# The last expert block of a mixture-of-experts layer: its rows by a product with a gate matrix, and one image's gathers beside that block

## The chip, the cores and the metric

One core of one Trainium2 chip. The time is device microseconds of one execution, and of several runs the median. A profile is one further execution, recorded by the hardware profiler; its times are microseconds from the start of its span.

## The reference

Four images of 384 channels and 32 x 32 pixels pass two layers: attention with tables of relative positions and a feed-forward net (layer 0), then convolutions channel by channel and a mixture of experts (layer 1). The change touches the mixture alone:

```python
scores = jnp.einsum('bsd,de->bse', x, gate_w) + gate_b
probs = jax.nn.softmax(scores, axis=-1)
topk_vals, topk_idx = jax.lax.top_k(probs, TOP_K)
mask = jnp.sum(jax.nn.one_hot(topk_idx, NUM_EXPERTS, dtype=probs.dtype), axis=-2)
masked = probs * mask
masked = masked / (jnp.sum(masked, axis=-1, keepdims=True) + 1e-09)
h = jax.nn.gelu(jnp.einsum('bsd,edh->ebsh', x, w1) + b1[:, None, None, :], approximate=False)
y = jnp.einsum('ebsh,ehd->ebsd', h, w2) + b2[:, None, None, :]
out = jnp.einsum('bse,ebsd->bsd', masked, y)
...
t = t + _L1_ffn_ref(_ln_t(t), ...)
```

A pixel is a token. Each of the 4096 tokens goes to two of four experts (384 to 1536 to 384), and the two results come back to it weighted by its two gates and are added to it.

## The kernel before, in words

Attention comes first (`qkv_phase`, `attention_phase`, to about 1490 us). Everything else is `rest_phase`: for each image the projection, the net of layer 0, the convolutions, the gates, and the experts.

*Dispatch.* When an image's gates are known, `scatter` writes each token's normalised row twice into the DRAM tensor `xs_d`, sorted by expert, with indirect DMAs on GpSimd. The index of a row is in `pos`; the two gates of a token are in `gate`. Both are tiles of 128 partitions with 8 x 2 values: partition p and column j stand for token 128 j + p, the last index for the first and the second expert.

*Blocks.* An expert works on blocks of 128 rows. There are 67 in all (`ALL`), since the blocks of each expert are rounded up; which expert a block has is data, and its weights are fetched by index. The 67 are in four groups, one after each image, of 13, 16, 16 and 22. `blocks` (L1252) runs through a group. For block k `fetch` gathers 128 rows into `xg` (L1258), `turn` transposes them on TensorE and copies them to `xT` (L1271, L1272), and twelve times three products give `e_ps` (L1309), ScalarE applies the Gelu (`eh`, L1312) and one product adds to `y_ps` (L1287). `y_ps` has two buffers. VectorE adds the bias, which stands at the end of the second half's weights, into `yo` (L1290, two buffers), and SyncE stores `yo` to 128 rows of the DRAM tensor `y_d` (L1292).

*Weights.* A block uses two halves of 128 x 4998 floats each, `wts[block % 2][half]`, fetched by an indirect DMA (`weights`, L1277) on GpSimd three halves ahead. A half whose buffer already holds the right expert is not moved. The second half's buffer is free only when `yo` of the block two before has been made.

*Combine.* `result_rows` (L803) turns an image's ranks into rows of `y_d` and puts them into `pos`. `combine` (L1324) then runs through quarters of 256 tokens: `results` gathers four tiles of 128 rows from `y_d` (L1348), `weigh` scales one by its gate on ScalarE (L1360) and adds the other, scaled, on VectorE (L1361), and `finish` transposes the sums on TensorE into `out_ps` (L1337), adds them to the residual on VectorE (L1338) and stores the result (L1339). For images 0 to 2 this starts at block 6 of the last group (`NOT_LAST`), by which all of their rows are in `y_d`, and is taken in steps beside the blocks. The fourth image may have rows in any block, the last one too; so `combine([B - 1])` stands behind the last block, with the whole of `y_d` as the source of its sixteen gathers. Its residual is still in SBUF (`xb`).

*Order.* GpSimd issues its DMAs in one queue, in the order of its instructions, and so does SyncE. The order on each engine is set when the program is built: a scheduler places instructions by its own estimate of when they are ready, except where `pin` (`keep_in_program_order`) holds them. `more` (L1483) is called after each twelfth of a block and hands out the other work in small steps, by a count of costs (`clock`). The tile `img` (128 x 3 x 38 x 38 floats) holds the padded image for the convolutions; the fourth image's convolution is its last reader.

Of the kernel before, what the change touches and what calls it, by code (L numbers as in the profile page):

```python
# [51 lines left out]

NOT_LAST = (2 * (B - 1) * N + NEXP * (BLK - 1)) // BLK - sum(COUNTS[:-1])
MAXB = B * N // BLK
OUTSIDE = 1e6


# [745 lines left out]
def result_rows(nc, small, image, pieces):  # L803


    shape = list(image["mask"].shape)

    def new(shape, name):
        return small.tile(shape, F32, tag=f"p_{name}", name=f"p_{name}", bufs=1)

    pos, part, step = new(shape, "pos"), new(shape, "prod"), new([P, 1, NEXP], "step")
    nc.vector.tensor_tensor(pos, image["rank"], bcast(pieces[0][1].unsqueeze(1), 1, shape[1]), ALU.add)
    for (_, off0), (lo, off) in zip(pieces, pieces[1:]):
        nc.vector.tensor_tensor(step[:, 0, :], off, off0, ALU.subtract)
        nc.vector.tensor_tensor(part, image["rank"], bcast(lo.unsqueeze(1), 1, shape[1]), ALU.is_ge)
        nc.vector.tensor_tensor(part, part, bcast(step, 1, shape[1]), ALU.mult)
        nc.vector.tensor_tensor(pos, pos, part, ALU.add)
    row = new([P, shape[1], 2], "fpos")
    for i, pick in enumerate(chosen(nc, new, image["mask"])):
        nc.vector.tensor_tensor(part, pick, pos, ALU.mult)  # L820
        nc.vector.tensor_reduce(row[:, :, i : i + 1], part, AX.X, ALU.add)
    nc.vector.tensor_copy(image["pos"], row)


def block_list(nc, small, cst, group, parts, done):
# [73 lines left out]
        nc.vector.tensor_tensor(done, done, took[:, turn], ALU.add)  # L899


def rest_phase(tc, cst, x, ao_d, ins, xs_d, y_d, x2_d, out):

# [6 lines left out]
    with ExitStack() as es:  # L912
# [339 lines left out]
        def blocks(g, more):  # L1252

            xT, xgs = {}, {}

            def fetch(k):
                xg = ld.tile([P, C], F32, tag="xg", name="xg")
                load = nc.gpsimd.indirect_dma_start(  # L1258
                    xg, None, from_xs, bass.IndirectOffsetOnAxis(ap=g["slot"][:, k, :], axis=0),
                    bounds_check=NEXP * CAP - 1, oob_is_err=False,  # L1260
                )
                for other in g["after"]:
                    after(load, other)
                xgs[k] = xg

            def turn(k):
                xg = xgs.pop(k)
                t = work.tile([P, KC, BLK], F32, tag="xT", name="xT")
                ps = ps_y.tile([P, KC, BLK], F32, tag="t", name="xT_ps")
                for c in range(KC):  # L1270
                    nc.tensor.transpose(ps[:, c, :], xg[:, c * P : (c + 1) * P], ident)  # L1271
                nc.scalar.copy(t, ps)  # L1272
                xT[k] = t

            def weights(k, fh):
                w = wts[(g["start"] + k) % 2][fh]
                nc.gpsimd.indirect_dma_start(  # L1277
                    w, None, ins["w12"], bass.IndirectOffsetOnAxis(ap=g["row"][:, k, fh : fh + 1], axis=0),
                    bounds_check=NEXP * 2 * P - 1, oob_is_err=False,
                )  # L1280
                return w

            pend = []

            def second(k, ff, hs, w, py):
                o = WB + ff % FH * C
                nc.tensor.matmul(py, hs, w[:, o : o + C], start=(ff == 0), stop=(ff == NF - 1))  # L1287
                if ff == NF - 1:
                    yo = hid.tile([P, C], F32, tag="yo", name="yo", bufs=2)
                    nc.vector.tensor_tensor(yo, py, w[:, WB + FH * C :], ALU.add)  # L1290
                    n = (g["start"] + k) * BLK
                    nc.sync.dma_start(y_d[n : n + BLK, :], yo)  # L1292


            fetch(0)
            ws = {h: weights(*divmod(h, 2)) for h in range(3)}
            turn(0)
            for k in range(g["nb"]):
                py = ps_y.tile([P, C], F32, tag="y", name="y_ps", bufs=2)
                for ff in range(NF):  # L1300
                    fh, f = divmod(ff, FH)
                    h = 2 * k + fh
                    w = ws[h]
                    if ff == 0 and k + 1 < g["nb"]:
                        fetch(k + 1)
                    ph = ps_h.tile([P, BLK], F32, tag="h", name="e_ps")
                    for c in range(KC):
                        o = c * FH * P + f * P
                        nc.tensor.matmul(ph, w[:, o : o + P], xT[k][:, c, :], start=(c == 0), stop=(c == KC - 1))  # L1309
                    hs = hid.tile([P, BLK], F32, tag="eh", name="eh")  # L1310
                    o = KC * FH * P + f
                    nc.scalar.activation(hs, ph, AF.Gelu, bias=w[:, o : o + 1])  # L1312
                    pend.append((k, ff, hs, w, py))
                    if len(pend) > 2:
                        second(*pend.pop(0))
                    if f == 2 and h + 3 < 2 * g["nb"]:
                        ws[h + 3] = weights(*divmod(h + 3, 2))
                    if ff == NF // 2 and k + 1 < g["nb"]:
                        turn(k + 1)
                    more(k)  # L1320
            for p in pend:
                second(*p)

        def combine(bs):  # L1324


            w = 2 * P
            end = bs[-1] == B - 1
            y_rows = y_d if end else y_d[: (groups[-1]["start"] + NOT_LAST) * BLK]
            pieces = [p for g in groups for p in g["pieces"]]  # L1330

            def finish(b, n0, xr, zs):
                for c0, c1 in ((0, 2), (2, 3)):
# [7 lines left out]
            def results(b, n0):  # L1341

                zs = []
                for j in range(2):
                    ys = [new_row() for _ in range(2)]
                    for i, y in enumerate(ys):
                        index = images[b]["pos"][:, n0 // P + j, i : i + 1]
                        nc.gpsimd.indirect_dma_start(y, None, y_rows, bass.IndirectOffsetOnAxis(ap=index, axis=0))  # L1348
                    zs.append(ys)
                if end:  # L1350
                    return zs, xbs[b][:, :, n0 : n0 + w]
                t0 = b * N + n0
                xr = ld.tile([P, KC, w], F32, tag="xr", name="xr")
                nc.sync.dma_start(xr, x2_d[:, t0 : t0 + w].rearrange("(k p) n -> p k n", p=P))
                return zs, xr

            def weigh(b, n0, zs):
                for j, (z, y) in enumerate(zs):
                    gate = images[b]["gate"][:, n0 // P + j, :]
                    nc.scalar.activation(z, z, AF.Copy, scale=gate[:, 0:1])  # L1360
                    nc.vector.scalar_tensor_tensor(z, y, gate[:, 1:2], z, ALU.mult, ALU.add)  # L1361
                return [z for z, _ in zs]

            if not end:
                for b in (*bs, B - 1):
                    result_rows(nc, small, images[b], pieces)
                    yield 3.0, 0.0
            todo = [(b, n0) for b in bs for n0 in range(0, N, w)]
            ahead = {}
            for i, (b, n0) in enumerate(todo):  # L1370
                for more in todo[i : i + (len(todo) if end else 2)]:
                    if more not in ahead:
                        ahead[more] = results(*more)
                zs, xr = ahead[b, n0]
                for _ in range(0 if end else 5):
                    yield 0.3, 0.0
                zs = weigh(b, n0, zs)
                for _ in range(0 if end else 5):
                    yield 0.3, 0.1
                finish(b, n0, xr, zs)  # L1380

        xbs, marks = {}, {}

# [99 lines left out]
        def more(g, k):  # L1483
            clock[0] += 0.05
            clock[1] += 1.36
            if g is groups[-1] and k == NOT_LAST and "combined" not in g:
                g["combined"] = combine(range(B - 1))
            spend(g.get("combined", iter(())))
            while clock[0] < clock[1] and spend(todo):
                pass  # L1490

        for i, g in enumerate(groups):
            blocks(g, lambda k: more(g, k))
            if i + 1 < len(groups):
                while "after" not in groups[i + 1]:
                    next(todo)
        for _ in groups[-1]["combined"]:
            pass
        for _ in combine([B - 1]):
            pass  # L1500


# [1 line left out]
def metaformer_kernel(ctx: ExitStack, tc: tile.TileContext, ins, out):  # L1504
# [14 lines left out]
    ao_d = [dram.tile([C, B, YT * IMG], F32, name=f"ao_d{i}") for i in range(2)]  # L1519
    x2_d = dram.tile([C, NT], F32, name="x2_d")  # L1520
    xs_d = dram.tile([NEXP * CAP, C], F32, name="xs_d")
    y_d = dram.tile([ALL * BLK, C], F32, name="y_d")

    with tc.tile_pool(name="held", bufs=1) as pool:
# [3 lines left out]
        ]  # L1528
        qkv_phase(tc, cst, ins["x"], ins["w_qkv"], qk_d, v_d)
        attention_phase(tc, cst, held, ins["tabs"], ins["tv"], qk_d, v_d, ao_d, xs_d, list(range(HEADS)))  # L1530
    rest_phase(tc, cst, ins["x"], ao_d, ins, xs_d, y_d, x2_d, out)


def attn_tables(table_q, table_k, table_v):
# [68 lines left out]
```

## Time and profile before

| | |
|---|---|
| median of 3 runs | 3050.28 us (3049.36 to 3055.75) |
| profiled execution, own time | 3065.37 us |
| its span | 3063.6 us |
| mean granted TensorE clock | 0.977 |
| TensorE busy | 2923.0 us, 95% of the span |
| VectorE busy | 1960.3 us, 64% |
| ScalarE busy | 1369.9 us, 45% |
| GpSimd busy | 1150.8 us, 38% |
| DMA | 500.56 MB, mean 163 GB/s |
| last `yo` starts | 3031.21 us |
| gathers of the combine step | 64, about 0.96 us each on GpSimd |

A line of a timeline has the start, the duration, the engine, the line of the kernel, the operation and its tiles (out<-in), and in brackets how long the engine had been idle before it and what ended that. PE is TensorE, DVE VectorE, ACT ScalarE, POOL GpSimd, SPq SyncE's queue. A duration on SPq or POOL of a DMA is that of its issue, not of the transfer. In a table of windows each row is one stretch of time: its length, the busy time of each engine with the number of instructions, the granted clock, the busy share of the 16 DMA engines, and GB/s.

### The profile page before, as it was taken

The page shows a single profiled execution, that of the slowest core. Times are in us where ns is not written, and L with a number is a line of the kernel's source. Part 1 is how long each engine was busy: PE and PEld are TensorE (multiplying, and loading weights), DVE is VectorE, ACT ScalarE, POOL GpSimd, SP SyncE. Part 2 cuts the span into 40 slices and gives each one's busy share as a digit, 9 for nine tenths or more (in the row PEclk, how much of TensorE's full clock was granted, in tenths as well). Part 3 has the DMA queues.
Part 4 walks back from the last instruction along what each step waited for, and adds up shares of the span by engine and source line. Part 5 has one row for each costly group of instructions (what it writes and reads, how often), then busy time and mean ns, then how long its engine had stood idle before and what let it go on. Part 6 is the DMA issues. An engine that isn't in the chain of part 4 may idle for free.

```text
span 3063.6 us, 63474 instructions
## 1 busy us (share of the span) xinstructions
PE 2923.0 (95%) x25391; PEld 2018.1 (66%) x25391; DVE 1960.3 (64%) x3577; ACT 1369.9 (45%) x2833; POOL 1150.8 (38%) x1123
## 2 busy tenths in 40 slices
PE   9988999999999999999899789999999999999996
PEld 4545777777777777777533347776577767777775
DVE  3227787878787878787478879999899540001101
ACT  1115767666766666666312232433342343233332
POOL 1114646464747473747300212251124231124412
PEclk9998999999999999999999889999999999999998
DMA  4446676767666676665400305724243165356742
GB/s 158 139 134 199 156 222 158 220 159 217 166 212 170 203 177 203 171 209 153 171 21 34 142 19 191 275 108 152 100 162 126 34 227 220 138 219 249 263 183 73
DMA packets 274568, 500.56 MB, mean 163 GB/s; under 512 B 135632, under 2 KB 204112, under 8 KB 266592
## 3 DMA queue, kind: packets, MB, share of 16 engines
q1 hardware_dynamic: 186576, 272.29, 29.0%
q0 software_dynamic: 37792, 202.68, 17.9%
q10 hardware_dynamic: 49904, 21.53, 3.6%
q8 instruction: 200, 3.28, 0.5%
q14 instruction: 96, 0.79, 0.1%
HBM read 543.58 MB, written 152.37 MB: 227 GB/s over the span
## 4 chain that ended last, share of the span: by engine, by line
PE 74%; DVE 13%; issue 6%; DMA 3%; ACT 2%; POOL 2%; SPq 0%; another core or an unknown queue 0%; DVEq 0%; POOLq 0%; ACTq 0%
PE e_ps L1309 12%; PE y_ps L1287 12%; DVE xb L1097 8%; PE t_ps L406 8%; PE sc_ps L221 7%; PE av_ps L221 7%; PE tabq_ps L221 6%; PE qk_ps L174 4%; PE a_ps L416 4%; PE tv_ps L221 2%; PE v_ps L185 2%; PE proj_ps L985 1%; PE tabk_ps L221 1%; PE tap_ps L1145 1%; PE f_ps L1020 1%
## 5 line engine op out<-in xcount | busy, mean ns | idle before, releaser
L1309 PEld LDWEIGHTS e_ps<-xT,w 128*128 128x128 f32 x4824 | 656.4, 193 | 215.1 <-issue 12.2
L349 POOL TENSOR_TENSOR bias<-b,s 128x416 f32<-128x416 f32 (+24 forms) x656 | 659.9, 1042 | 176.6 <-DMA s<-sd 160.5
L1309 PE MATMUL e_ps<-xT,w 128*128 128x128 f32 x4824 | 670.7, 277 | 11.7 <-DVE xb L1038 5.0
L1287 PE MATMUL y_ps<-w,eh 128*128 128x384 f32 x1608 | 652.4, 491 | 15.6 <-ACT eh L1312 12.8
L1097 DVE SCALAR_TENSOR_TENSOR xb<-img,pack,xb 128x1024 f32<-128x1024 f32 (+1 forms) x539 | 634.6, 1241 | 0.0
L1312 ACT ACTIVATE eh<-e_ps,w 128x128 f32<-128x128 f32 x804 | 292.8, 367 | 724.3 <-PE e_ps L1309 665.3
L1277 POOL DMA_INDIRECT w<-in_w,row x134 | 169.2, 1263 | 743.6 <-PE y_ps L1287 276.8
L398 DVE TENSOR_REDUCE extra<-arow 128x32 f32<-128x32 f32 (+24 forms) x768 | 381.7, 556 | 9.0 <-ACT arow L387 5.4
L377 DVE CUSTOM_DVE_ANT_0 arow<-sc_ps,bias 128x1024 f32<-128x1024 f32 x256 | 312.8, 1222 | 101.3 <-issue 52.5
L387 ACT ACTIVATE arow<-arow,nm 128x1024 f32<-128x1024 f32 x256 | 302.2, 1180 | 77.0 <-DVE nm L377 66.8
L406 PEld LDWEIGHTS t_ps<-ident,arow 128*128 128x128 f32 x2048 | 220.4, 142 | 173.6 <-ACT aT L407 100.6
L407 ACT COPY aT<-t_ps 128x512 f32<-128x512 f32 x512 | 278.5, 603 | 92.8 <-PE t_ps L406 91.3
L406 PE MATMUL t_ps<-ident,arow 128*128 128x128 f32 x2048 | 282.3, 281 | 15.6 <-ACT arow L387 15.6
L1290 DVE TENSOR_TENSOR yo<-y_ps,w 128x384 f32<-128x384 f32 x67 | 37.0, 553 | 394.8 <-PE y_ps L1287 389.9
L221 PE MATMUL sc_ps<-kk,qs 48*32 48x512 f32 x4096 | 277.6, 605 | 6.6 <-DVE nm L377 5.6
L1287 PEld LDWEIGHTS y_ps<-w,eh 128*128 128x128 f32 x1608 | 248.3, 193 | 30.6 <-ACT eh L1312 17.2
L221 PEld LDWEIGHTS av_ps<-aT,vb 128*64 128x64 f32 x4096 | 222.3, 137 | 51.3 <-ACT aT L407 41.2
L221 PE MATMUL av_ps<-aT,vb 128*64 128x128 f32 x4096 | 237.7, 274 | 0.0
L314 DVE STREAM_TRANSPOSE b<-tabk_ps 128x480 f32<-128x480 f32 x256 | 218.5, 982 | 23.7 <-PE tabk_ps L221 22.2
L221 PE MATMUL tabk_ps<-tab,kq 48*128 48x480 f32 x512 | 223.3, 583 | 8.2 <-DVE b L314 8.2
L221 PE MATMUL tabq_ps<-tab,kq 48*128 48x480 f32 x512 | 220.4, 579 | 2.1 <-ACT aT L407 1.5
L318 ACT COPY st<-tabq_ps 128x480 f32<-128x480 f32 x256 | 142.3, 560 | 74.8 <-PE tabk_ps L221 46.3
(210 smaller groups left out, 3140.3 us busy)
## 6 DMA issues: line engine op xcount, KB each, us to landing
sd<-st SPq DMA_DIRECT2D x128, 480.0 KB
s<-sd SPq DMA_DIRECT2D x256, 240.0 KB
xs_d<-zero SPq DMA_DIRECT2D x64, 384.0 KB
tvw<-in_tv SPq DMA_DIRECT2D x120, 192.0 KB
y_d<-yo SPq DMA_DIRECT2D x67, 192.0 KB
qk_d<-qk_sb POOLq DMA_DIRECT2D x48, 256.0 KB
qs<-qk_d SPq DMA_DIRECT2D x256, 48.0 KB
kq<-qk_d ACTq DMA_DIRECT2D x56, 192.0 KB
```

Of the source, the lines that this page charges most:

```text
L221: ins = nc.tensor.matmul(*args, **kw)
L314: turn = nc.vector.transpose(b2.rearrange("p e y x -> p x (e y)")[:, i + j], ps[:, j, : SPAN * IMG])
L349: nc.gpsimd.tensor_tensor(bias[:, y0:y1, :], bass.AP(b2.tensor, b2.offset + (e * IMG + y0) * IMG, [list(b2.ap[0]), [(step * IMG + 1) * IMG ...
L377: nc.vector.tensor_tensor_reduce(s["flat"], ps.rearrange("p h n -> p (h n)"), s["bias"].rearrange("p y x -> p (y x)"), -SCALE, BIG, ALU.ad ...
L387: nc.scalar.activation(s["flat"], s["flat"], AF.Exp, bias=s["nm"], scale=-1.0, accum_out=dn[:, y % YT : y % YT + 1])
L398: pin(nc.vector.tensor_reduce(ex[:, i, :], a[:, p0:p1, :].rearrange("p y x -> p x y"), AX.X, ALU.add))
L406: pin(nc.tensor.transpose(pt[:, j, :], s["flat"][:, k0 : k0 + P], ident))
L407: pin(nc.scalar.copy(aT[:, 4 * g : 4 * g + 4, s["y"] % YB, :], pt))
L1097: ins_ = nc.vector.scalar_tensor_tensor(acc[:, k, y0:y1], img[:, k, dy + y0 : dy + y1, dx : dx + IMG], w7[:, k, dy, dx : dx + 1], acc[:, k ...
L1287: nc.tensor.matmul(py, hs, w[:, o : o + C], start=(ff == 0), stop=(ff == NF - 1))
L1309: nc.tensor.matmul(ph, w[:, o : o + P], xT[k][:, c, :], start=(c == 0), stop=(c == KC - 1))
L1312: nc.scalar.activation(hs, ph, AF.Gelu, bias=w[:, o : o + 1])
```

## The change

The last block's `yo` is not stored. All other blocks' rows are still gathered from `y_d`; only rows below `LAST` (66 x 128) count. A gather of a row at or above it is left out by a bounds check on the index, and its gate is set to zero in a copy of the gates, `kept`. The contribution of the last block reaches its tokens in another way: `picked` is a matrix of 128 rows (of the block) by 1024 tokens with a token's gate where that token's result is this row, and zero elsewhere. For a quarter of the image and each 128 channels, the product of `yo` and `picked` starts a sum in PSUM, to which the transposed weighted rows are added by products with the identity. An addition then takes the sum to the residual.

`picked` is made by `choose`: the distance of each token's row from `LAST` (`rel`) and the gates go as single floats to a small DRAM tensor `pick_d` of 4 x 1024, and come back broadcast over all partitions (512 KB each). One VectorE step of 128 x 1024 for each of the two experts compares the distance with the partition's number and multiplies by the gate, and a third adds the two. The four tiles of 1024 floats lie in `img`. `choose` is taken in steps with the quarters of images 0 to 2; in the built order its first VectorE steps follow the fourth image's `result_rows`, ahead of block 36's `yo`.

The sixteen gathers of the fourth image are issued once the last block but one has made its `yo`, that is in the program beside the last block. Weighing and the sums come after the last block, as before; the two instructions of `weigh` are pinned.

```diff
+LAST = (ALL - 1) * BLK
...
                     n = (g["start"] + k) * BLK
-                    nc.sync.dma_start(y_d[n : n + BLK, :], yo)
+                    g["result"] = k, yo
+                    if n < LAST:
+                        nc.sync.dma_start(y_d[n : n + BLK, :], yo)
...
+        kept = small.tile([P, nj, 2], F32, tag="e_kept", name="e_kept", bufs=1)
+        room = img.rearrange("p k y x -> p (k y x)")
+        picked, other, where, weight = (room[:, i * N : (i + 1) * N] for i in range(4))
+
+        def choose(row):
+            gate = images[B - 1]["gate"]
+            rel = small.tile([P, nj, 2], F32, tag="e_rel", name="e_rel", bufs=1)
+            nc.vector.tensor_scalar_add(rel, row, -float(LAST))
+            nc.vector.tensor_scalar(kept, rel, 0.0, None, ALU.is_lt)
+            nc.vector.tensor_tensor(kept, kept, gate, ALU.mult)
+            yield 0.5, 0.0
+            for i in range(2):
+                for j, src in enumerate((rel, gate)):
+                    nc.sync.dma_start(pick_d[2 * i + j].rearrange("(j p) -> p j", p=P), src[:, :, i])
+                yield 0.0, 0.0
+            for i in range(2):
+                for dst, j in ((where, 0), (weight, 1)):
+                    nc.sync.dma_start(dst, bass.AP(pick_d.tensor, pick_d.offset + (2 * i + j) * N, [[0, P], [1, N]]))
+                yield 0.0, 0.0
+                nc.vector.scalar_tensor_tensor(
+                    other if i else picked, where, pc["wrow"][:, 0:1], weight, ALU.is_equal, ALU.mult
+                )
+            nc.vector.tensor_tensor(picked, picked, other, ALU.add)
...
-            y_rows = y_d if end else y_d[: (groups[-1]["start"] + NOT_LAST) * BLK]
+            y_rows = y_d[:LAST] if end else y_d[: (groups[-1]["start"] + NOT_LAST) * BLK]
...
+            def close(b, n0, xr, zs):
+                yo = groups[-1]["result"][1]
+                sums = []
+                for c, (pool, tag) in enumerate(((ps_m, "m"), (ps_h, "h"), (ps_y, "y"))):
+                    ps = pool.tile([P, TOK], F32, tag=tag, name="out_ps", **({"bufs": 2} if tag == "y" else {}))
+                    nc.tensor.matmul(
+                        ps[:, :w], yo[:, c * P : (c + 1) * P], picked[:, n0 : n0 + w], start=True, stop=False
+                    )
+                    sums.append(ps)
+                for j in range(2):
+                    for c, ps in enumerate(sums):
+                        nc.tensor.matmul(
+                            ps[:, j * P : (j + 1) * P], zs[j][:, c * P : (c + 1) * P], ident,
+                            start=False, stop=(j == 1),
+                        )
+                for c, ps in enumerate(sums):
+                    nc.vector.tensor_tensor(xr[:, c, :], xr[:, c, :], ps[:, :w], ALU.add)
+                nc.sync.dma_start(out[b, :, n0 : n0 + w].rearrange("(k p) n -> p k n", p=P), xr)
...
-                        nc.gpsimd.indirect_dma_start(y, None, y_rows, bass.IndirectOffsetOnAxis(ap=index, axis=0))
+                        bound = {"bounds_check": LAST - 1, "oob_is_err": False} if end else {}
+                        nc.gpsimd.indirect_dma_start(
+                            y, None, y_rows, bass.IndirectOffsetOnAxis(ap=index, axis=0), **bound
+                        )
...
-                    gate = images[b]["gate"][:, n0 // P + j, :]
-                    nc.scalar.activation(z, z, AF.Copy, scale=gate[:, 0:1])
-                    nc.vector.scalar_tensor_tensor(z, y, gate[:, 1:2], z, ALU.mult, ALU.add)
+                    gate = (kept if end else images[b]["gate"])[:, n0 // P + j, :]
+                    keep = pin if end else lambda ins_: ins_
+                    keep(nc.scalar.activation(z, z, AF.Copy, scale=gate[:, 0:1]))
+                    keep(nc.vector.scalar_tensor_tensor(z, y, gate[:, 1:2], z, ALU.mult, ALU.add))
...
             spend(g.get("combined", iter(())))
+            if g is groups[-1] and g.get("result", (0,))[0] == g["nb"] - 2 and "tail" not in g:
+                for _ in g["combined"]:
+                    pass
+                g["tail"] = combine([B - 1])
+                next(g["tail"])
...
-        for _ in groups[-1]["combined"]:
-            pass
-        for _ in combine([B - 1]):
+        for _ in groups[-1]["tail"]:
             pass
```

## What was predicted, before the changed kernel had been run

> **What bounds the kernel now.** I read the timeline of the last 64 us first, because the change ends there, then the chain of waits over the same stretch; then the timelines of VectorE, GpSimd and SyncE around 2515 us, because the order of instructions in the two built programs puts the new preparation there; last a table of windows and the waits of SyncE's queue. The tail, by instruction:
>
> ```profile
> 3016.77 0.56 DVE L1290 TENSOR_TENSOR yo<-y_ps,w 128x384 f32<-128x384 f32 x1 [15.74 <-PE y_ps L1287]
> ...
> 3031.21 0.56 DVE L1290 TENSOR_TENSOR yo<-y_ps,w 128x384 f32<-128x384 f32 x1 [13.89 <-PE y_ps L1287]
> 3034.43 0.97 POOL L1348 DMA_INDIRECT rows<-y_d,pos  x1 [31.64 <-DMA y_d<-yo]
> ...
> 3053.43 0.96 POOL L1348 DMA_INDIRECT rows<-y_d,pos  x1 [0.30 <-issue]
> ...
> 3056.04 0.61 ACT L1360 ACTIVATE rows<-rows,gate 128x384 f32<-128x384 f32 x1 [1.86 <-DMA rows<-y_d,pos]
> ...
> 3057.24 0.62 DVE L1361 SCALAR_TENSOR_TENSOR rows<-rows,gate 128x384 f32<-128x384 f32 x1
> ...
> 3058.85 1.02 DVE L1338 TENSOR_TENSOR xb<-xb,out_ps 128x512 f32<-128x512 f32 x2 [0.99 <-PE out_ps L1337]
> ```
>
> TensorE bounds all but the end. After the last block's `yo` at 3031.21 come 32.4 us in which it is nearly idle. In them the store of `yo` must land before GpSimd may issue the first of 16 gathers (3.22 us after `yo` starts); the sixteen take 19.00 us from first to last start, 1.27 us each; and from the last one's start to the end it is 10.17 us. Two `yo` lie 14.44 us apart here.
>
> The second place, where the kernel is not short of anything that costs time yet:
>
> ```profile
> 2511.98 1.04 POOL L1277 DMA_INDIRECT w<-in_w,row  x1 [1.59 <-remote]
> ...
> 2514.21 0.19 DVE L821 TENSOR_REDUCE p_fpos<-p_prod 128x8 f32<-128x32 f32 x1
> 2519.26 0.56 DVE L1290 TENSOR_TENSOR yo<-y_ps,w 128x384 f32<-128x384 f32 x1 [4.87 <-PE e_ps L1309]
> ...
> 2521.00 1.05 POOL L1277 DMA_INDIRECT w<-in_w,row  x1 [0.30 <-issue]
> ...
> 2530.46 1.02 POOL L1258 DMA_INDIRECT xg<-xs_d,slot  x1 [0.30 <-issue]
> ...
> 2546.21 0.49 PE L1271 MATMUL xT_ps<-ident,xg 128*128 128x128 f32 x3
> ```
>
> ```profile
> 2516.00:2520.00 4.00, 4.00 (x27) 3.20 (x26) 0.56 (x1) 0.76 (x3) 3.09 (x4) 1.00 1.05 375
> ...
> 2536.00:2540.00 4.00, 4.00 (x26) 3.20 (x25) 0.64 (x2) 1.10 (x3) 1.00 (x1) 1.00 0.97 343
> ...
> 2548.00:2552.00 4.00, 4.00 (x27) 3.20 (x26) 0.00 (x0) 1.10 (x3) 0.00 (x0) 1.00 0.14 42
> ```
>
> The last two columns are the DMA engines' busy share and GB/s. From 2516 to 2546 the 16 DMA engines are full: a new expert begins at block 38, and four halves of weights of 2.5 MB each (blocks 38 and 39) pass, with scatters of 192 KB between. TensorE is still busy throughout, but with little margin: the rows `xg` of block 39, issued at 2530.46 behind two of these halves, landed by the single packets' records at about 2540, and are transposed at 2546.21.
>
> ```profile
> 2814.91 0.38 SPq L1339 DMA_DIRECT2D out<-xr  x1
> 2834.04 0.36 SPq L1354 DMA_DIRECT2D xr<-x_d  x1
> ```
>
> This is what a SyncE transfer meets in such a stretch: the load waits for the store ahead of it to land, which took 19 us for 24 packets of 1 KB per engine; between 2773.09 and 2776.77 the same pair took 3.7 us.
>
> **What the Trainium skill says.** "DMA: Bandwidth & Descriptors", section "Queues, rings and completion order": every DMA engine takes its queue rows in turn, packet by packet. The trace agrees: at 2812 to 2814 the records hold 33 weight packets of 19,992 bytes (about 0.7 us each) and 40 of SyncE's queue, one for one. The same page, "Why a DMA increments its semaphore by 16 and not by 1": one descriptor moves one contiguous run, so a store of single floats has a descriptor per float; no run here shows 4-byte data, but the loads of 128-byte runs at 48.9 us show 1536 packets in 1.22 us, 13 ns each per engine. "TensorE: Matmul & The Clock Gate", Part 1: the clock halves after an idle window of about 3.4 us; the windows table agrees (clock 0.66 in 3032 to 3036, then 0.50).
>
> **The tail, removed and moved.** The gathers of the fourth image no longer need the last block's store. They wait for block 65's, whose `yo` starts at 3016.77; GpSimd is free from 3002.8. First gather 3016.77 + 3.22 = 3019.99, last start 3038.99. They lie beside the last block, in windows where the DMA engines are all but idle (share 0.00 to 0.14), so it pays nothing. The scaling stays behind the last `eh` on ScalarE and the last `yo` on VectorE by program order.
>
> New work after `yo` ends at 3031.77: per quarter of the image three products of 128x256, six of 128x128, two weighings and three additions of 128x256. The products need `yo` and a buffer alone and start at once, about 0.2 us each (128x384 starts every 0.33); they lie beside the weighings. A quarter costs VectorE: two weighings 1.15 (starts 0.53 apart, the last 0.62), about 0.5 from the last weighing to the first sum (0.99 before, for a bank of four products at half clock), three additions 1.07 (the short one is 0.41): 2.75. If VectorE alone set the end: 3031.77 + 4 x 2.75 + 3.73 (end of the last addition 3059.87 to 3063.6) = 3046.5. The gathers are later: the last lands 3.1 to 3.9 after its start (first gather to first scaling 3.16; fifteenth 3.87), so with 3.8 the last weighing starts at 3042.8, ends 3043.4, additions 3044.0 to 3045.1, end 3048.8. **Gain 14.8**; bounds 14.4 (a pure shift by one block) to 15.5. The store dropped is off the path; the check on the indices is at 1.01 us for `xg` against 0.96, which the 0.3 us gaps absorb or 16 x 0.05 = 0.8 cost.
>
> **The preparation, added.** In the built order the three small VectorE steps (0.16 us each) follow the last reduction at 2514.21, and the first 128x1024 step stands before block 36's `yo` (2519.26). It waits for: positions ready 2514.6, two stores of 1024 single floats on SyncE's queue (64 packets per engine each), then a broadcast load of 512 KB. Behind it in VectorE wait `yo` of block 36, and behind that on GpSimd the weights of block 38's second half (2521.00 waits for this `yo`, since `yo` reads the bias in that buffer), two scatters, the first half of 39 and `xg` of 39. The two gate stores and the first load stand earlier, at 2495 to 2502, where the DMA share is 0.2 to 0.3: nothing.
>
> When does that first step go? The store starts about 2515.6 (1 us, as `yo`'s store shows). Until about 2525 GpSimd's queue still holds half of block 38 and six scatters: about 6 weight packets and 18 scatter packets per engine, so one for one 24 of the 64 floats pass. The other 40 then need 0.5 to 1.4 us (13 to 36 ns each, the spread of 128-byte packets), 2526; landing and SyncE's issue 2 us, the second store's 64 packets in front; 8 x 4 KB per engine at 0.16 us is 1.3; landing about 1: 2530.3. The step takes 1.24 (L1097, same shape): `yo` at about 2531.5, twelve us late. Its own buffer allows that, since `y_ps` has two and block 38 reuses it at 2538.
>
> GpSimd then issues the weights at 2532.4 instead of 2521.0, into empty engines: first packets 1.4 later, half 38 in 6.4 (128 packets at about 40 per 2 us), two broadcasts and `yo` beside it 2.7, scatters 1, half 39 in 6.4, `xg` 0.5 and landing 0.8: 2551.6, against its use at 2546.2. **TensorE waits about 5 us**, and since it is 100% busy from 2548 on, the loss stays. As a rule: stall = `yo` of 36 minus 2526. Bounds: 0 if the floats slip through and `yo` is back before 2526; 14 if a float costs 0.1 us per engine instead of 0.02, which puts 104 of them 8 to 10 us later.
>
> The second step waits for the second index load, issued behind the stall's own weights: 8 packets at 0.75 is 6 us, so block 37's `yo` goes at about 2545 instead of 2536.8; its weights are needed after 2566. Nothing. Later products, orders of ScalarE, GpSimd and the gathers of images 0 to 2 are the same instruction for instruction.
>
> Sum: -14.8 + 5 = -9.8. On the profiled execution, 3065.37 (span 3063.6 and 1.8 around it): 3055.6. The shown runs' median is 15.1 below that execution for a reason the profile doesn't show; I take the same difference from it: 3050.28 - 9.8 = **3040.5**.
>
> **Rivals.** *No stall* (the floats are passed several per turn, or `xg` has more margin than I read): for it, TensorE shows no stall in that stretch today; against it, the 19 us store. 3050.28 - 14.8 = 3035.5. *A longer stall that eats most of the gain* (9 to 21 us: floats at 0.06 to 0.15 us, or the delayed weights of block 38 late as well): 3044.3 to 3056, middle 3050. *Slower*: single-float stores to HBM cost over 0.15 us per engine each. The place is the wait of VectorE's first 128x1024 step ahead of block 36's `yo`; it decides once that `yo` is later than about 2547 (2526 + 14.8 + 6.1). At 0.2 us the 104 floats left at 2525 take 21, then 5 for load and step, and landing: about 2553, stall 27, 3062. For it: the same skill page, "Specifications", says that below 512 bytes the engine reads, modifies and writes; against it, 128 packets of 128 bytes to HBM at 322.95 took 0.52 us. *The gathers don't move* (they still wait for a later transfer): tail gain about 1, stall 5, 3054; the built order has them behind the last weights with seven queue semaphores to wait for, all of stores up to block 65, so little speaks for it.
>
> **How the numbers follow.** Forecast with a stall of 2 to 8.7: 0.46, own range 3037.5 to 3044. No stall 0.19; longer stall 0.20; slower 0.11; gathers unmoved 0.04. What this kernel's measurement can tell from no change is about 0.2%, 6.1 us. Faster by more: 0.46 + 0.19 = 0.65. Within: the longer stall and the unmoved gathers, 0.24. Slower: 0.11. The range starts at 3033, below the no-stall case with its best tail (3050.28 - 15.5, less the runs' own spread of some us), and ends at 3055, which leaves out the slower case and the very end of the two before it.
>
> **What would show it.** Right: first gather of the tail about 3.2 us after block 65's `yo`; 17.6 us instead of 32.4 from the last `yo` to the end, set by the last gather; block 36's `yo` 10 to 14 us late with VectorE idle on the load of `img` before it; a gap of about 5 us in TensorE ahead of the `xT_ps` group that stood at 2546. Wrong: no such gap, or one that begins at `y_ps` of block 38 instead; a tail set by VectorE; a change of the block period between 2750 and 2935.

## The result and the profile after

The change made the kernel slower: 3065.85 us median of 6 runs (3063.98 to 3073.9) against 3050.21 us (6 runs, 3049.36 to 3055.75), a ratio of 1.0053 with a 95% interval of 1.0041 to 1.0065, or 13 to 20 us. The profiled execution has a span of 3070.4 us and an own time of 3072.18.

First the timeline of the changed kernel's tail:

```profile
3036.59 0.56 DVE L1292 TENSOR_TENSOR yo<-y_ps,w 128x384 f32<-128x384 f32 x1 [15.74 <-PE y_ps L1289]
...
3039.89 1.01 POOL L1399 DMA_INDIRECT rows<-y_d,pos  x1 [17.27 <-DMA y_d<-yo]
...
3051.04 0.56 DVE L1292 TENSOR_TENSOR yo<-y_ps,w 128x384 f32<-128x384 f32 x1 [13.89 <-PE y_ps L1289]
...
3060.09 1.01 POOL L1399 DMA_INDIRECT rows<-y_d,pos  x1 [0.30 <-issue]
...
3063.83 0.62 DVE L1415 SCALAR_TENSOR_TENSOR rows<-rows,e_kept 128x384 f32<-128x384 f32 x1 [1.78 <-ACT rows L1414]
...
3065.34 1.27 DVE L1379 TENSOR_TENSOR xb<-xb,out_ps 128x256 f32<-128x256 f32 x3 [0.89 <-PE out_ps L1374]
```

The tail does what it was meant to do. The first gather comes 3.30 us after the `yo` of the last block but one, nine of the sixteen start before the last block's `yo`, and from that `yo` to the end it is 3070.4 - 3051.04 = 19.4 us where it was 32.4. So 13.0 us are gained there, and 13 to 20 us more than that must be lost elsewhere.

They are lost around block 36. SyncE's queue and VectorE in the changed kernel's timeline:

```profile
2501.24 1.43 SPq L1343 DMA_DIRECT2D pick_d<-gate  x2
2517.49 0.33 SPq L1347 DMA_DIRECT2D img<-pick_d  x1
...
2527.36 1.71 SPq L1343 DMA_DIRECT2D pick_d<-e_rel  x2
2548.13 9.72 SPq L1347 DMA_DIRECT2D img<-pick_d  x2
```

```profile
2527.16 0.17 DVE L1337 TENSOR_SCALAR e_rel<-p_fpos 128x16 f32<-128x16 f32 x1
...
2556.21 1.28 DVE L1349 SCALAR_TENSOR_TENSOR img<-img,pack 128x1024 f32<-128x1024 f32 x1 [28.21 <-DMA img<-pick_d]
2557.41 0.55 DVE L1292 TENSOR_TENSOR yo<-y_ps,w 128x384 f32<-128x384 f32 x1
2567.59 1.28 DVE L1349 SCALAR_TENSOR_TENSOR img<-img,pack 128x1024 f32<-128x1024 f32 x1 [9.62 <-DMA img<-pick_d]
```

A load from `pick_d` is issued once the store that it reads has landed. The first gate store, 4 KB, takes from 2501.24 to 2517.49 for that, while little else gets through (2 to 39 GB/s in windows of 4 us from 2500 to 2520). The two stores of positions land 20.7 and 24.9 us after their issue, at 2548.07 and 2552.70. Weights pass beside them at first. But by the records of the single packets no packet of any queue begins from 2544 to 2550, and still the stores haven't landed. A row of a table of windows, with the engines in the order PE, PEld (TensorE's loading of weights), DVE, ACT, POOL:

```profile
2544.00:2548.00 4.00, 4.00 (x27) 3.20 (x26) 0.00 (x0) 1.10 (x3) 0.00 (x0) 1.00 0.00 0
```

The load behind them lands 3.5 us after the second. VectorE stands idle for 28.21 us ahead of its first step over 128x1024, and block 36's `yo` waits behind it. What this does to TensorE, again by the timeline:

```profile
2518.98 1.65 PE L1289 MATMUL y_ps<-w,eh 128*128 128x384 f32 x2 [6.11 <-ACT eh L1316]
...
2558.11 1.62 PE L1289 MATMUL y_ps<-w,eh 128*128 128x384 f32 x2 [8.26 <-DVE yo L1292]
...
2571.42 1.65 PE L1313 MATMUL e_ps<-xT,w 128*128 128x128 f32 x6 [6.55 <-DMA w<-in_w,row]
...
2579.41 0.52 PE L1273 MATMUL xT_ps<-ident,xg 128*128 128x128 f32 x3 [1.28 <-DMA xg<-xs_d,slot]
```

Four gaps, 22.2 us. The last three belong to the late `yo`: a buffer of `y_ps` that it holds, weights that GpSimd may issue only after it, and the rows behind these. The first has nothing to do with `yo`. It comes right after the gate stores, and on ScalarE it begins with this:

```profile
2518.56 0.37 ACT L1316 ACTIVATE eh<-e_ps,w 128x128 f32<-128x128 f32 x1 [9.17 <-remote]
```

"remote" is a release that the profile finds in no instruction of this program. The three longer gaps also leave TensorE at half clock for a while (granted clock 0.50 from 2520 to 2524 and from 2556 to 2560, 0.54 from 2572 to 2576).

To compare kernels I use the starts of `yo` on VectorE: between two of them the same work lies in each kernel, whatever an execution lost before. The stretch from the `yo` of block 34 (counted from 0, as in the prediction) to the last one holds all of the change but the tail. Each figure of this kind is from one profiled execution.

### The profile page after: what moved, and what is told of

Its sections match the earlier page's. It is cut to its first block, busy times and chain, and to the rows that moved or that the text cites. A ratio compares the mean times of both kernels' runs of the same rounds, so it can differ in the third digit from the quotient of the medians.

```text
span 3070.4 us, 63606 instructions
## 1 busy us (share of the span) xinstructions
PE 2933.3 (96%) x25439; PEld 2027.1 (66%) x25439; DVE 1964.7 (64%) x3587; ACT 1372.5 (45%) x2833; POOL 1158.1 (38%) x1123
## 4 chain that ended last, share of the span: by engine, by line
PE 74%; DVE 13%; issue 5%; DMA 4%; POOL 2%; ACT 2%; SPq 1%; POOLq 0%; DVEq 0%; ACTq 0%
PE e_ps L1313 12%; PE y_ps L1289 12%; DVE xb L1099 8%; PE t_ps L407 7%; PE sc_ps L222 7%; PE av_ps L222 7%; PE tabq_ps L222 5%; PE qk_ps L175 4%; PE a_ps L417 3%; PE tv_ps L222 2%; PE v_ps L186 2%; PE tabk_ps L222 2%; DMA s<-sd 1%; PE proj_ps L987 1%; PE tap_ps L1147 1%
## 5 line engine op out<-in xcount | busy, mean ns | idle before, releaser
L1289 PEld LDWEIGHTS y_ps<-w,eh 128*128 128x128 f32 x1608 | 249.3, 193 | 33.9 <-ACT eh L1316 14.7
L1215 POOL DMA_INDIRECT xs_d<-rows,pos x64 | 78.6, 1229 | 259.9 <-DVE b_first L851 228.1
```

## The experiments

Ratios are against runs of the kernel before on the same chip in the same comparison. There its medians were 3051 to 3053 us with single runs from 3041 to 3061, so the ratio is the figure to read; 0.001 is 3.05 us.

| kernel | ratio, 95% interval | us from `yo` 34 to the last `yo` | against 543.77 |
|---|---|---|---|
| before, first profile | 1 | 560.77 | +17.0 |
| before, second profile | 1 | 543.77 | 0 |
| changed kernel | 1.0053 (1.0041 to 1.0065) | 573.57 | +29.8 |
| tail_only | 0.9945 (0.9926 to 0.9963) | 543.59 | -0.2 |
| prepare_only | 1.0085 (1.0064 to 1.0106) | 571.74 | +28.0 |
| late_steps | 0.9998 (0.9986 to 1.0010) | 553.42 | +9.7 |
| runs_64b | 0.9976 (0.9966 to 0.9986) | 551.96 | +8.2 |
| runs_late | 0.9975 (0.9961 to 0.9988) | 545.38 | +1.6 |
| rows_late | 0.9958 (0.9944 to 0.9972) | 543.98 | +0.2 |
| gate_floats | 1.0036 (1.0021 to 1.0051) | 553.93 | +10.2 |
| gate_spread | 0.9994 (0.9984 to 1.0003) | 543.76 | 0.0 |
| gate_pitch64 | 0.9999 (0.9988 to 1.0010) | 543.96 | +0.2 |

**The kernel before, once more.**

> The kernel before, for a second profile. All profiles since have the blocks 50 to 60 quicker by 13.4 us than the first profile of the kernel before, with the old tail and with the new one, and blocks 35 to 37 quicker by 4 where nothing is added. If that belongs to the one execution first profiled, this profile shows the quick blocks: from yo of block 50 to that of block 60 171.7 us instead of 185.1, from 34 to 38 78.7 instead of 82.4. If the kernel before is always so, it shows the same as the first.

The second profile shows the quick blocks (span 3043.1, own time 3044.89). The first had lost 17.0 us in this stretch that no later profile of any kernel loses. So the changed kernel's loss is measured against the second: 29.8 us. With the tail's 13.0 that makes +16.8, inside the 13 to 20 of the timed runs.

**Which half of the change costs?** tail_only:

```diff
-            for i in range(2):
-                for j, src in enumerate((rel, gate)):
...
-            nc.vector.tensor_tensor(picked, picked, other, ALU.add)
+            nc.vector.memset(picked, 0.0)
```

> The changed kernel without its preparation: the stores, loads and steps that build the matrix of gates are left out, and the matrix is set to zero, so the last block adds nothing to the fourth image; the moved gathers and the new products stay. Theory F (the loss lies in the preparation, in the stores of single floats): the tail keeps what its trace shows, 32.4 - 19.4 = 13.0 us, and nothing is lost at block 36: 3050.2 - 13.0 = 3037, between 3035 and 3039. Rival R (part of the loss lies in the moved gathers or in the new tail, not in the preparation): 3042 or more.

prepare_only: the kernel before with `pick_d`, `kept`, `choose` and this call of it, and nothing else of the change:

```diff
+                if not end:
+                    next(chooser, None)
                 zs, xr = ahead[b, n0]
```

> The kernel before with the preparation added and its result not used: the last block's rows are stored and gathered as before. Theory F: 26 us lost about block 36 and nothing won: 3076, between 3073 and 3080; the gate stores again take about 15 us until the load behind them is issued. Theory C (my prediction's: floats pass one for one with weight packets): a loss of 5 us, 3055, at most 3064. Rival R (part of the loss belongs to the moved gathers): between 3060 and 3072.

Both came out as theory F has it: 0.55% faster (17 us, interval 11 to 23), a little below the stated 3035 in its median of 3034.48, and 0.85% slower (26 us, 20 to 32; median 3076.89). The preparation carries the whole loss, and the moved gathers and the new products carry none.

**Late data, or blocked engines?** late_steps lets the same floats go out at the same places, but nothing on VectorE waits for them until block 55:

```diff
+            got = [room[:, i * N : (i + 1) * N] for i in range(4)]
...
+            key = small.tile([P, 1], F32, tag="e_key", name="e_key", bufs=1)
...
+            nc.vector.scalar_tensor_tensor(
+                key, groups[-1]["result"][1][:, 0:1], 0.0, pc["wrow"][:, 0:1], ALU.mult, ALU.add
+            )
...
-                    other if i else picked, where, pc["wrow"][:, 0:1], weight, ALU.is_equal, ALU.mult
+                    got[2 * i], got[2 * i], key, got[2 * i + 1], ALU.is_equal, ALU.mult
```

> The changed kernel with the same four stores of single floats, but the two steps over 128x1024 on VectorE stand some twenty blocks later, behind a later block's yo, and both pairs of rows have a place of their own. Theory H (the stores only make data late; the loss is VectorE waiting ahead of block 36's yo): that wait goes and all of the 26 us with it: 3037, at most 3040. Theory B (the stores also hold up everything else that the DMA engines write, and with it the other engines): the loss at the gate stores stays, 6 us of TensorE's stall and some at half clock, and the second pair of stores still holds up weights: 3043 to 3056.

Neither theory alone. The wait ahead of `yo` is worth 29.8 - 9.7 = 20 us, and 9.7 us stay without it, as theory B said. Its timeline shows where:

```profile
2490.73 1.43 SPq L1343 DMA_DIRECT2D pick_d<-gate  x2
...
2504.52 0.37 ACT L1316 ACTIVATE eh<-e_ps,w 128x128 f32<-128x128 f32 x1 [5.50 <-remote]
2506.98 4.64 SPq L1349 DMA_DIRECT2D img<-pick_d  x2
...
2515.27 1.22 SPq L1343 DMA_DIRECT2D pick_d<-e_rel  x2
2549.11 8.36 SPq L1349 DMA_DIRECT2D img<-pick_d  x2
...
2562.17 0.56 DVE L1292 TENSOR_TENSOR yo<-y_ps,w 128x384 f32<-128x384 f32 x1 [20.55 <-DMA y_d<-yo]
```

The second of the two loads at 2506.98 waits for the second gate store and is issued at 2511.29: that store took 19.5 us. About half of the 9.7 comes before block 36 (its `yo` is 5.4 us further from block 34's than in the second profile of before), behind the "remote" wait. The other half comes at block 38: its `yo` waits for the store of an earlier `yo`, which stands on SyncE's queue behind the loads that wait for the floats. The first of the two stores of positions took 33.8 us among the weights, the second 41.4; by the records of the packets, weights and floats pass about one for one there (40 of each from 2532 to 2534). Out of VectorE's way, the wait had gone into the next queue.

**The number of floats?** runs_64b writes 128 runs of 64 bytes twice, instead of 1024 single floats four times. The steps still stand ahead of a `yo`, but in the built order the first has moved by one block, from ahead of block 36's to ahead of block 37's:

```diff
+            for j, src in enumerate((rel, gate)):
+                nc.vector.tensor_copy(line[:, :, j, :], src.rearrange("p j i -> p i j"))
...
-                    nc.sync.dma_start(pick_d[2 * i + j].rearrange("(j p) -> p j", p=P), src[:, :, i])
+                nc.sync.dma_start(flat[i].rearrange("(p c) -> p c", p=P), line[:, i].rearrange("p s j -> p (s j)"))
```

> The changed kernel with the four stores of 1024 single floats made into two stores of 128 runs of 64 bytes (VectorE first puts a partition's positions and gates side by side), one load of 8 KB per partition for each of the two steps, and the steps ahead of block 36's yo as in the changed kernel. Theory F (the number of floats costs): the stores take below 2 us, the first step waits only for a load that passes weight packets, the stall is 0 to 6 us: 3037 to 3043. Theory Q (what makes the data late is SyncE's queue and the full DMA engines, not the floats): the stall stays at 15 us or more: 3052 or more.

```profile
2518.06 0.81 SPq L1346 DMA_DIRECT2D pick_d<-e_line  x2
2521.27 0.56 DVE L1292 TENSOR_TENSOR yo<-y_ps,w 128x384 f32<-128x384 f32 x1 [3.10 <-PE y_ps L1289]
2526.31 0.32 SPq L1351 DMA_DIRECT2D img<-pick_d  x1
...
2539.60 2.02 DVE L1354 SCALAR_TENSOR_TENSOR img<-img,pack 128x1024 f32<-128x1024 f32 x1 [17.77 <-DMA img<-pick_d]
2549.54 2.00 DVE L1354 SCALAR_TENSOR_TENSOR img<-img,pack 128x1024 f32<-128x1024 f32 x1 [7.92 <-DMA img<-pick_d]
...
2552.72 0.55 DVE L1292 TENSOR_TENSOR yo<-y_ps,w 128x384 f32<-128x384 f32 x1
```

Runs in place of floats take away 29.8 - 8.2 = 21.6 us of the loss, and the changed kernel turns into one faster than before (0.9976). A part of the 21.6 belongs to the shift, since block 36's `yo` at 2521.27 no longer waits. Ahead of it, the step would have held it until 2541.6, which is 2537.5 on the clock of the prediction; by the prediction's rule that is an estimate of 11.5 us lost instead of 8.2. Theory F's time is too low all the same: the first store took 8 us among the weights, not 2, and the first load (8 KB for each of 128 partitions) another 13 us from its issue to the step. This is the kind of wait that my prediction had described, and it costs 8.2 us here.

**The fourth corner.** runs_late has the runs of runs_64b and the late steps of late_steps. Both loads keep a place of their own, the steps work in place, and one copy on VectorE more puts the sum into the order of the tokens.

> runs_64b with its stores and loads at the same place and the steps over 128x1024 behind a later block's yo, as in late_steps. With the changed kernel, late_steps and runs_64b it fills the square of two causes: stores of floats or of runs, steps ahead of yo or behind. Theory H (what runs_64b still loses, some 8 us about blocks 36 to 39, is VectorE waiting ahead of yo): the loss goes, ratio 0.9957 as in rows_late, yo of 34 to 39 within 1 us of the kernel before. Rival Q (the broadcast loads among the weights delay weights and rows by themselves): 5 us or more stay, ratio 0.9972 or more.

By the trace 1.6 us stay, which is theory H: all but 1.6 of the 8.2 was VectorE waiting ahead of `yo`. What stays is for the most part one wait of TensorE for rows `xg` (1.34 us), issued among the loads. The timed ratio of 0.9975 lies on rival Q's side of the line that I had drawn. It stands for 7.6 us gained where the trace leads one to expect 13.0 - 1.6 = 11.4, and the interval (4 to 12) just reaches that. Whether runs_late loses something more that its one profile doesn't show stays open.

So the square is, in us lost: floats and early steps 29.8, floats and late steps 9.7, runs and early steps 8.2 (early by a block less), runs and late steps 1.6. The two causes are more than a sum, since the slower stores are, the longer the wait ahead of `yo`.

**What is it about the floats?** gate_floats is the kernel before with the two gate stores alone. gate_spread and gate_pitch64 send the same 2048 floats from the same places, 512 and 64 bytes apart instead of 4 (shown for 64, against gate_floats; 512 has 128 in place of the 16):

```diff
-                nc.sync.dma_start(pick_d[2 * i + 1].rearrange("(j p) -> p j", p=P), gate[:, :, i])
+                nc.sync.dma_start(
+                    pick_d[2 * i + 1].rearrange("(j p) c -> p j c", p=P)[:, :, 0:1], gate[:, :, i : i + 1]
+                )
...
-    pick_d = dram.tile([4, N], F32, name="pick_d")
+    pick_d = dram.tile([4, N, 16], F32, name="pick_d")
```

> The kernel before with nothing added but the two stores of the gates, 1024 single floats each, at the place where the changed kernel has them; nothing reads them. Theory F: the 2048 floats take about 14 us from their issue to the landing of the second, scatters' packets meanwhile take microseconds each, ScalarE waits 3 us or more on a release that is not from this core's program, and the kernel loses 5 to 9 us: ratio 1.0015 to 1.003. Theory C (13 to 36 ns per float): landed in 3 to 5 us, nothing lost, ratio within 0.001 of 1.

> As gate_floats, but the floats go to addresses 512 bytes apart instead of side by side. Theory F1 (a single float costs by itself): as slow as gate_floats, 14 us or more. Theory F2 (the cost comes from several DMA engines writing into the same short stretch of memory at once): landed in 5 us or less and nothing lost.

> As gate_spread with the floats 64 bytes apart instead of 512. Floats 512 bytes apart cost nothing and floats side by side cost about 11 us. If a stretch of 64 bytes is what engines must not share, this is as quick as gate_spread: landed in about 3 us, ratio within 0.001 of 1. If the stretch is longer (512 bytes, as the place where the Trainium skill's DMA page sets a limit for small descriptors), the loss stays in whole or in part: ratio 1.0015 or more.

DMA issues in 28 us from shortly before the stores (out<-in, queue, operation, count, KB each, median us from issue to landing), gate_floats first and then gate_pitch64:

```profile
y_d<-yo SPq DMA_DIRECT2D x1, 192.0 KB, 13.5
xs_d<-rows,pos POOLq DMA_INDIRECT x8, 11.2
```

```profile
xs_d<-rows,pos POOLq DMA_INDIRECT x13, 5.0
y_d<-yo SPq DMA_DIRECT2D x1, 192.0 KB, 2.1
...
pick_d<-gate SPq DMA_DIRECT2D x2, 4.0 KB, 2.9
```

And tables of windows, 4 us each, of gate_floats and of gate_pitch64:

```profile
2508.00:2512.00 4.00, 3.67 (x24) 2.81 (x22) 1.89 (x12) 0.20 (x1) 2.62 (x3) 1.00 0.55 17
2512.00:2516.00 4.00, 0.00 (x0) 0.00 (x0) 0.00 (x0) 0.00 (x0) 2.32 (x3) 1.00 0.63 22
2516.00:2520.00 4.00, 0.67 (x1) 0.50 (x2) 1.72 (x13) 1.00 (x3) 0.00 (x0) 0.59 0.81 71
```

```profile
2508.00:2512.00 4.00, 4.00 (x26) 3.20 (x25) 3.72 (x28) 1.15 (x4) 0.82 (x1) 1.00 0.19 71
2512.00:2516.00 4.00, 4.00 (x25) 3.17 (x25) 3.71 (x30) 1.17 (x4) 3.08 (x4) 1.00 0.37 128
2516.00:2520.00 4.00, 4.00 (x25) 3.15 (x24) 3.62 (x26) 1.15 (x4) 3.08 (x4) 1.00 0.41 150
```

The same floats, the same queue, the same moment. Side by side they cost 11 us (ratio 1.0036; 10.2 in the trace), more than the 5 to 9 expected; 64 or 512 bytes apart they land in 2.9 us and cost nothing. For the gate stores it is thus neither the number of floats nor their size, but their addresses. For the stores of positions this was not run by itself: runs_64b took away their number and their nearness together. In gate_floats a store of `yo` of 192 KB takes 13.5 us instead of 2.1, the DMA engines are 0.55 to 0.81 busy and move 17 to 71 GB/s, and for 4 us TensorE, VectorE and ScalarE all stand still, though SyncE alone has to do with these stores.

**A version that is faster than both.** rows_late takes floats and waits away:

```diff
+            nc.tensor.transpose(turned[: 4 * nj, :P], line.rearrange("p i s j -> p (i s j)"), ident)
+            rows = small.tile([4 * nj, P], F32, tag="e_rows", name="e_rows", bufs=1)
+            nc.vector.tensor_copy(rows, turned[: 4 * nj, :P])
+            nc.sync.dma_start(pick_d.rearrange("a (j p) -> (a j) p", p=P), rows)
```

> The changed kernel with another way to the same matrix of gates: VectorE puts positions and gates side by side, TensorE transposes the 32 columns, one store writes 32 runs of 512 bytes, two loads bring 8 KB per partition, and the three steps over 128x1024 stand behind a later block's yo, as in late_steps. Theory F+H (the loss is the stores of single floats and the wait that stands ahead of yo; both are gone here): only the tail's gain is left, about 13 us below the kernel before (ratio 0.9957; 0.994 to 0.997), and no gap over 1 us in TensorE in the stretch of blocks 35 to 39. Rival Q (any load of 512 KB broadcast over all partitions holds up weights): 5 us or more lost wherever the loads fall, ratio 0.998 or more.

```profile
2771.76 0.42 SPq L1348 DMA_DIRECT2D pick_d<-e_rows  x1
2775.72 0.81 SPq L1353 DMA_DIRECT2D img<-pick_d  x2
...
2853.19 2.48 DVE L1363 SCALAR_TENSOR_TENSOR img<-img,e_key 128x1024 f32<-128x1024 f32 x2
```

The ratio is 0.9958 (median 3038.73), 8.5 to 17 us faster than before, as expected; 0.2 us are lost on the way to the last `yo`. The loads are issued 4 us after the store, and the matrix is ready at 2857, 166 us before the first product with it. Store and loads stand some 250 us later than in the other kernels, but among other transfers too (DMA share 0.87 to 1.02 from 2772 to 2788). The loads of 1 MB each cost nothing here; rival Q, which had them cost 5 us wherever they fall, falls. What the transposition, the runs of 512 bytes and the later place are each worth, this kernel doesn't separate.

## Why the prediction was wrong

3040.5 us were predicted (range 3033 to 3055), and 3065.85 came. The rival called slower stood at 3062 with a chance of 0.11, and it came nearest: it had block 36's `yo` at about 2553. It put that down to the price of a single float, though, and floats 64 bytes apart cost nothing.

- *The tail: right, 1.8 us too good.* Predicted were 17.6 us from the last `yo` to the end, and it took 19.4. The gathers follow each other mostly at 1.31 us instead of 1.27 (some take 1.23 to 1.28 instead of 1.01), so the last starts 23.50 us after block 65's `yo` instead of 22.2; and the last sums begin 0.9 us after the weighing instead of 0.5 and take 1.27 instead of 1.07. The last gather sets the end, as predicted.
- *"The two gate stores and the first load stand earlier, at 2495 to 2502, where the DMA share is 0.2 to 0.3: nothing."* **This step failed.** Alone they cost 11 us (gate_floats). I had looked for other traffic that could hold them up, and never asked what they would hold up themselves.
- *"40 then need 0.5 to 1.4 us (13 to 36 ns each, the spread of 128-byte packets)".* **The same error in the other pair.** In the records the floats are even cheaper than that (a median of 7 ns for the gates, 9 for the positions); it is the landing that is dear. The first gate store took 16.2 us with little beside it, and the second landed 20.5 us after the first was issued (late_steps); at 64 floats per engine and store (1024 over 16) that is 0.16 us for each of 128. The bound that I had set for the slower rival, 0.15, was met. The packet of 128 bytes was the wrong row to take the price from, because the price, of the gate stores at least, hangs on what lies next to the float in memory.
- *The wait ahead of block 36's `yo`, and GpSimd's weights behind it: right in part.* `yo` of block 36 came at 2557.41 in an execution that was by then 7 us later, so at about 2550 on the clock of the prediction. The rule "stall = `yo` of 36 minus 2526" then gives 24, with what the gate stores did to this `yo` already in it. The trace has 29.8 against the second profile, and 26.2 against the execution that the rule was read from, which lost 3.6 there itself. So the rule was usable and its input was off by 19 us: the first store of positions was issued 5 us later than predicted, and from there to the landing of the load it took 28.8 us instead of 14.7. The place was not the one forecast. Behind this `yo` TensorE stopped first at `y_ps` of block 38 (8.26 us), which the prediction had named as a sign of being wrong, then for the weights of block 38 (6.55), and only 1.28 us ahead of the `xT_ps` group where about 5 had been forecast.
- *One for one with the weight packets: right in kind, small.* The records show it in late_steps (40 and 40 packets in 2 us) and in runs_64b, where 30 packets of the load pass beside 31 of weights from 2532 to 2534. With runs instead of floats it is the wait that is left, and costs 8.2 us, one block later, instead of the 5 put down for it.
- *"The shown runs' median is 15.1 below that execution for a reason the profile doesn't show; I take the same difference".* That was sound. The second profile shows the reason's place: 17.0 us lost between blocks 34 and 60 of the one execution first profiled.
- *Later products and orders unchanged:* right; from block 38 on the distance to the second profile of the kernel before stays at 40.05 to 40.07 us up to the last `yo`.

## What to carry to other kernels

Small values that change from a column of partitions into a row should be stored in runs, put side by side by VectorE (runs_late) or transposed by TensorE first (rows_late, the fastest here): two stores of single floats at neighbouring addresses cost ten microseconds here with little other traffic, and stopped engines that had no part in them. A step that waits for a DMA is better placed behind the instructions that hand buffers back, on every queue that it stands in: on VectorE it held `yo`, and out of VectorE's way its loads held the stores of `yo` on SyncE. And where the profiled execution is off its own median, a second profile of the same kernel is worth more than an argument on the first.

## What had not been expected of the hardware

- The records of the single packets give 7 to 9 ns to each of the 2048 gate floats, spaced or not. The time appears in others: the 31 scatter packets that begin from 2502 to 2506 in gate_floats take 3.5 and 9.1 us in the mean of each 2 us (the longest 11.7), where those of the same size behind the floats of gate_pitch64 take 0.20. A cheap packet in the records is no proof of a cheap store: in the changed kernel the last floats of positions are recorded before 2544, and their second store landed at 2552.70.
- The Trainium skill, "DMA: Bandwidth & Descriptors", section "Back-pressure in remote DMA", says of transfers between cores that stalled writes stall a DMA engine's other queues too. Here it happens within one core, with writes to DRAM: queue after queue slows down. That several engines write into one short stretch of memory fits with the distances of 4, 64 and 512 bytes, and with the same page's "Specifications", which gives eight partitions to an engine: the 16 floats of 64 neighbouring bytes come from 16 partitions, and so from two engines at least. But the records don't name the engine of a packet, and distances between 4 and 64 bytes were not tried, so this is argued.
- The limit of 512 bytes, which the Trainium skill gives in "DMA: Bandwidth & Descriptors", section "Specifications", with reading and modifying below it, doesn't decide here: stores of 4 bytes, 64 bytes apart, landed in 2.9 us and cost nothing that can be measured.
- TensorE, VectorE and ScalarE stopped for 4 us together. In gate_floats the next packet of an instruction queue comes 20.2 us after the stores' issue, in gate_pitch64 9.0; that the engines had run out of instructions fits this and the trace's "remote", but no run separates it from other reasons.
